# A four-image scan network on one core: a deeper head, spaced background loads and a staggered end

## The chip, the cores and the metric

The kernel runs on one core of a Trainium2 chip. The core has five engines that run side by side: TensorE (PE in the profile, with PEld for its weight loads), VectorE (DVE), ScalarE (ACT), GpSimd (POOL) and SyncE (SP), which here only starts transfers. Each engine works through its own list of instructions in order. On-chip data lies in SBUF, results of matmuls in PSUM, inputs and scratch tensors in DRAM; transfers between them are asynchronous.

The metric is the device time of one execution in microseconds (us). The kernel before takes 5479.21 us, the median of three runs from 5474.62 to 5479.99.

## The reference

The input is 4 images of 64 x 64 positions with 96 channels. Per image there is a convolution branch with a state-space scan, then a linear attention and a feed-forward layer with rounding. Cut to what matters here:

```python
xp, z = split(bilinear(group_norm(x), W_in, s_in, b_in))     # signs of x times signs of W
t = conv3x3(sign(xp + move), s * sign(conv_W)) + biases      # 192 -> 192 channels
t = where(t >= 0, t, prelu * t) + rp_b1 + xp
xconv = silu(t)                                              # "u" in the kernel
x_hwwh = stack([xconv by rows, xconv by columns])            # and both reversed: 4 directions
xs = concat([x_hwwh, flip(x_hwwh)])
dts, Bs, Cs = split(bilinear(xs as rows of 192, Wl, sl, bl)) # per direction
h = exp(dt * A) * h + (dt * u) * B                           # along 4096 positions, 192 x 16 states
y = sum_n(h * C) + D * u
y = y_0 + flip(y_2) + (y_1 + flip(y_3)) by columns turned back to rows
y = layernorm(y) * silu-like gate of z;  x = x + bilinear(y, W_out, ...)
t = x + attention(layernorm(x))      # linear: q (k^T v), summed over the whole image
t = t + ffn(layernorm(t))            # 96 -> 384 -> 96, rounded to small float formats
```

Two things shape the kernel. The attention sums k^T v over the whole image, so the end of an image has a first pass (sums), a small middle product and a last pass. And the scan of a direction needs, for each position, the rows B, C and dt that are made from the whole convolution.

## The kernel before

The main loop, `Scans.run`, goes through 1536 pieces (4 images, 4 directions in the order 1, 3, 0, 2, 4 stretches of 1024 positions, 6 groups of 32 channels, 4 groups of states). Each piece is a decay on ScalarE, an input product on GpSimd, a scan on VectorE, a product with C on VectorE or GpSimd, and a reduction on TensorE. All other work, the head of the next images and the end of the finished ones, is written as Python generators; after each piece one step of them is emitted, so that it fills the engines' gaps:

```python
for i in range(n):
    self.loads(i)
    ...
    if i % NQ == 1:
        while KORD[self.pieces[i][1]] == 2 and self.pieces[i][0] not in c.turned:
            next(back)                       # forced: the turned sums are needed now
        self.load_sums(i)
    self.carry(i - 1); self.decay(i + 1)     # ScalarE
    self.reduce(i - 4)                       # TensorE
    self.inject(i + AHEAD); self.late_product()   # GpSimd
    self.scan(i)                             # VectorE
    c.later.tick()                           # stores that were put off
    ...
    interleave(lanes)                        # one step of the next deltas (dps)
    next(back, None)                         # one step of the background work
```

The background, in `run`: for each image b in turn, wait until its second direction is scanned, turn that direction's result from columns to rows (`turn`), make the head of image b + 2 (`prologue`), then sums, middle and last of image b.

```python
scans = Scans(c)
...
    for b in range(NB):
        while not scans.done(b, 2): yield
        yield from turn(c, b)
        if b + 2 < NB: yield from prologue(c, b + 2)
        e = ends[b]; e.open()
        yield from e.sums(e.lane)
        if b + 1 < NB:
            yield from e.middle(); yield from e.last(e.lane); e.close()
...
drain([e.middle()])                                       # image 3, after the scans
drain([e.last(ln) for ln in [e.lane] + more])             # four lanes, one step each in turn
```

Image 0's head has no scan beside it (`alone`). It runs in turn with `weights()`, which prepares all weights: `interleave([made, first])`. Its convolution works on 16 parts of 512 columns (two halves h of the channels, eight q). Each part, in four steps and an ending:

```python
for n, part in enumerate(parts + [None]):
    for s in range(4):
        if part: ...                               # 15 matmuls "cv", four to a step
        if ahead and s == 0: next(ahead[0])        # projection of a later part: matmuls ix, iz
        if ahead and s == 2: next(ahead.pop(0), None)   # its signs tp, sz on ScalarE
        if prev and s == 0: pz = pz * S_X + v; pz = r * oma + pz     # VectorE, two products
        if prev and s == 1: sign(ph, pq, pz); e = exp(-pz)           # ScalarE
        if prev and s == 2: e = ln(1 + e); e = exp(-e)               # ScalarE
        if prev and s == 3: u = pz * e                               # VectorE
                            c.later.store(ud, u); by_columns(ph, pq, u)   # GpSimd copy into ut
        yield
    if part:
        v = cv * acs + acb                         # VectorE
        r = relu(cv * csc + cbias)                 # ScalarE
        pz = winT.T @ xsT                          # TensorE, "cz"
        prev = (h, q, pz, v, r, nm)
```

`sign` stores its 32-row pieces with `c.later.store(xgw[...], sg[m::3, :])`, a transfer started by SyncE two steps later. The tile ut for u by columns comes from a pool that closes at the end of the convolution.

Then the rows stage turns xg into xr (13 copies, banks used in turn of two), makes B, C and dt (acc, eight row products), and writes bcd and the signs sgd. `Scans.start` begins with loads of u and of the B rows (bc), makes the first deltas and sends them on as dl.

The parts of the background with a load ahead of a use:

```python
load_x(c, b, xts); yield; yield                    # prologue: then the column sums (csum)
...
c.later.flush()                                    # end of the convolution: last signs to xg
with tc.tile_pool(name=f"rw_{b}", bufs=1) as rw:   # rows: xg read, xr written at once
...
ts = [load(*part) for part in parts[:3]]           # turn: three loads ahead of the copies (yh)
...
if (ci, part) == (NCH - 1, 0) and k != KORD[-1]:   # deltas: signs of the next direction,
    self.load_signs(b, KORD[KORD.index(k) + 1])    #   but not of the next image
...
tt = ln.tts[n % 2]; nc.sync.dma_start(tt[0:96, :], c.td[b][...])   # last: then the product "at"
```

In the last pass each chunk of 512 columns goes through: at, x2, fc, square, fv, rstd, t8, three hidden products hp, fy, fo, ft, out. A step is about one of these.

Of the kernel before, what the change touches and what calls it, by code (L numbers as in the profile page):

```python
# [53 lines left out]
def hybrid_kernel(ctx: ExitStack, tc: tile.TileContext, a: dict, out: bass.AP):  # L54
# [108 lines left out]
    def weights():  # L163
# [110 lines left out]
        part = temp("part", [96, 2, 2])  # L274
        for i, cut in enumerate(cuts):
            nc.scalar.activation(cwA.rearrange("p t d -> p (t d)")[:, cut], cfa[i], AF.Sign, saturate=False)
            nc.scalar.activation(cwB[:, lines[i]], cfb[i], AF.Sign, saturate=False)
            for h in range(2):
                nc.vector.tensor_reduce(part[:, h, i : i + 1], cwn[h][i], AX.X, ALU.add, apply_absolute_value=True)
        nc.vector.tensor_tensor(csc, part[:, :, 0], part[:, :, 1], ALU.add)  # L280
        nc.vector.tensor_scalar(csc, csc, 1.0 / (9 * DN), None, ALU.mult)
        yield

        nc.vector.tensor_tensor(cbias, pv[:, :, CONV_B], pv[:, :, RP0], ALU.add)
        nc.vector.tensor_tensor(acs, pv[:, :, PRELU], csc, ALU.mult)
        nc.vector.tensor_tensor(acb, pv[:, :, PRELU], cbias, ALU.mult)
        nc.vector.tensor_tensor(acb, acb, pv[:, :, B_X], ALU.add)
        nc.vector.tensor_tensor(acb, acb, pv[:, :, RP1], ALU.add)
        nc.vector.tensor_scalar(oma, pv[:, :, PRELU], -1.0, 1.0, ALU.mult, ALU.add)
        for h in range(2):  # L290
            nc.gpsimd.tensor_scalar(omad[:, h], i96, oma[:, h : h + 1], None, ALU.mult)
        yield
# [5 lines left out]
        for o in range(2):  # L298
# [18 lines left out]
            yield  # L317

# [87 lines left out]

def load_x(c, b, xts):
    src = c.a["x"][b].rearrange("(i p) e -> p i e", p=128)
    for q, t in enumerate(xts):
        c.nc.sync.dma_start(t, src[:, 8 * q : 8 * q + 8, :])  # L410
# [41 lines left out]
def run(c):  # L452

    made, first = c.weights(), prologue(c, 0, c.xts)
    lanes = [made, first]
    next(made)
    for _ in range(6):
        next(first)
    while (0, 1) not in c.ready:
        interleave(lanes)  # L460
        c.later.tick()
    assert made not in lanes
    scans = Scans(c)
    ends = [Epilogue(c, b, scans) for b in range(NB)]

    def back():
# [3 lines left out]
        for b in range(NB):  # L470
            while not scans.done(b, 2):
                yield
            yield from turn(c, b)
# [5 lines left out]
            if b + 1 < NB:  # L479
                yield from e.middle()  # L480
                yield from e.last(e.lane)
                e.close()
# [15 lines left out]
    more.append(e.fourth_lane())  # L498
    drain([e.middle()])
    drain([e.last(ln) for ln in [e.lane] + more])  # L500
# [3 lines left out]
def prologue(c, b, xts=None):  # L504
# [11 lines left out]
    with tc.tile_pool(name=f"xg_{b}", bufs=1) as xgp:  # L516
# [3 lines left out]
        with tc.tile_pool(name=f"cv_{b}", bufs=1) as cvp:  # L520
# [7 lines left out]
            if xts is None:  # L528
# [5 lines left out]
                yield  # L534
                yield

            csum = bank("csum", 0)[0:1, 0 : 4 * DM]
            for i in range(0, NT, 4):
# [4 lines left out]
                if i % 8 == 4:  # L543
                    yield
            row = f32("csr")[0:1, 0 : 4 * DM]
# [98 lines left out]
            utp = sub.enter_context(tc.tile_pool(name=f"ut_{b}", bufs=1))  # L644
            uts = {}

            def by_columns(h, q, u):


                per = 2 if alone and h else 4  # L650
                if q % per == 0:
                    uts[h] = utp.tile([96, IW, 8 * per], F32, name=f"ut{h}{q}_{b}", tag=f"ut{h if alone else 0}")
# [3 lines left out]
                if q % per == per - 1:  # L656
                    rows = slice(8 * (q + 1 - per), 8 * q + 8)
                    c.later.store(c.utd[b][h].rearrange("p (w h) -> p w h", h=IH)[:, :, rows], ut, after=1)

            def sign(h, q, pz):  # L660
# [5 lines left out]
                for m in range(3):  # L666
                    g0 = 64 * (m // 2) + 32 * h
                    c.later.store(xgw[g0 : g0 + 32, m % 2, 128 * q : 128 * q + 128], sg[m::3, :])

            for n, part in enumerate(parts + [None]):  # L670
                if part:
                    h, q = part
                    nm = f"{h}{q}"
                    if alone:
                        ps = c.p.dA.tile([128, CH], F32, name=f"cv{nm}_{b}", tag="dA")[0:96, 0:512]
                    else:
                        ps = bank("cv" + nm, 0)[0:96]
                for s in range(4 if alone else 5):
                    if part:
                        per = 4 if alone else 3  # L680
                        for tp, w, dy, dx in taps[per * s : per * s + per]:
# [4 lines left out]
                    if alone and ahead:  # L686
                        if s == 0:
                            next(ahead[0])
                        elif s == 2:
                            next(ahead.pop(0), None)  # L690
# [3 lines left out]
                    if prev:  # L694
                        ph, pq, pz, v, r, pn = prev
                        if s == 0:
                            if alone:
                                c.vec.scalar_tensor_tensor(pz, pz, pv[:, ph, S_X : S_X + 1], v, ALU.mult, ALU.add)
                                c.vec.scalar_tensor_tensor(pz, r, c.oma[:, one(ph)], pz, ALU.mult, ALU.add)
                            else:  # L700
                                nc.scalar.mul(pz, pz, pv[:, ph, S_X : S_X + 1])
                        elif s == 1 and not alone:
# [3 lines left out]
                        elif s == (1 if alone else 2):  # L706
# [4 lines left out]
                        elif s == (2 if alone else 3):  # L711
                            nc.scalar.activation(e, e, AF.Ln, bias=1.0)
                            nc.scalar.activation(e, e, AF.Exp, scale=-1.0)
                        elif s == (3 if alone else 4):
# [4 lines left out]
                            if alone:  # L719
                                by_columns(*turned)  # L720
                                turned = None
                    yield
                if part:
                    v, r = f32("v" + nm)[0:96], f32("r" + nm)[0:96]
                    if alone:
                        nc.vector.tensor_scalar(v, ps, c.acs[:, one(h)], c.acb[:, one(h)], ALU.mult, ALU.add)
                    else:
                        nc.scalar.activation(v, ps, AF.Identity, scale=c.acs[:, one(h)], bias=c.acb[:, one(h)])
                    nc.scalar.activation(r, ps, AF.Relu, scale=c.csc[:, one(h)], bias=c.cbias[:, one(h)])  # L729
                    pz = bank("cz" + nm, n % 2 if alone else 1)[0:96]  # L730
# [11 lines left out]

        with tc.tile_pool(name=f"rw_{b}", bufs=1) as rw:
# [7 lines left out]
            gw = g2.bitcast(F32)  # L751
            for o in (1, 0):
# [10 lines left out]
                for n in range(13):  # L763
# [3 lines left out]
                    if n < 8:  # L767
                        ps = bank(f"xa{o}{n}", n % 2)
# [3 lines left out]
                    elif n < 12:  # L772
                        ps = bank(f"xb{o}{n}", n % 2)
# [9 lines left out]
                for gh in range(2):  # L783
                    groups = slice(32 * gh, 32 * gh + 32)
                    prev = None
                    for n in range(5):
# [9 lines left out]
                        if n < 4:  # L796
                            acc = prev = bank(f"acc{o}{gh}{n}", n % 2)
# [36 lines left out]
                for x, k in enumerate((o, o + 2)):  # L834
                    nc.sync.dma_start(gw[:, x, 16:64], c.sgd[b][k].rearrange("(p f) -> p f", p=128))
                    yield
# [25 lines left out]
def turn(c, b):  # L862
# [9 lines left out]
    with tc.tile_pool(name=f"tn_{b}", bufs=1) as tn:  # L872
        ts = [load(*part) for part in parts[:3]]
        for n, (h, q) in enumerate(parts):
            if q == 0:
                yh = tn.tile([96, L], F32, name=f"yh{h}_{b}", tag=f"yh{h}")
# [5 lines left out]
            if n + 3 < len(parts):  # L882
                ts.append(load(*parts[n + 3]))
# [5 lines left out]
class Epilogue:  # L889


    def __init__(self, c, b, scans):
        self.c, self.b, self.scans = c, b, scans

        self.todo, self.rest = list(range(NQ8))[::-1], list(range(NQ8))
# [83 lines left out]
    def loads(self, ln, q, names):  # L979
        c, b = self.c, self.b  # L980
        cols = slice(512 * q, 512 * q + 512)
        for nm in names:
# [6 lines left out]
            c.nc.sync.dma_start(t[0:96], src[..., cols])  # L989
# [162 lines left out]
    def last(self, ln):  # L1152
# [21 lines left out]
        x1 = residual(nxt[0]) if nxt else None  # L1174
        while nxt:
# [73 lines left out]
class Scans:  # L1249
# [20 lines left out]
    def done(self, b, n):  # L1270

        return self.at > (b * NK + n) * NPC + SETTLE
# [14 lines left out]
    def prepare(self, spare=None):  # L1287
# [11 lines left out]
        if (ci, part) == (NCH - 1, 0) and k != KORD[-1]:  # L1299
            self.load_signs(b, KORD[KORD.index(k) + 1])  # L1300
# [168 lines left out]
    def evacuate(self, i):  # L1469
# [6 lines left out]
        c.nc.scalar.copy(t, y[:, :, ::-1] if k >= 2 else y)  # L1476
        at = CH * (NCH - 1 - ci if k >= 2 else ci)
# [4 lines left out]

    def start(self):
# [3 lines left out]
        w = [p.w.tile([128, CH], F32, name=f"w_s{x}", tag="w") for x in range(8)]  # L1487
        t, d2, us = w[4:6], w[6], w[2:4]
# [177 lines left out]
```

## Time and profile before

The page says of the whole span of 5482.3 us:

| engine | busy us | share |
|---|---|---|
| VectorE | 5016.3 | 91% |
| GpSimd | 4938.7 | 90% |
| ScalarE | 3615.3 | 66% |
| TensorE, matmuls | 3415.9 | 62% |

By time the span falls into three: a head until about 257 us, in which image 0 is prepared; the scans until about 5352 us; and the end of image 3, about 130 us. In the page's 40 slices of 137 us GpSimd shows 2, 3, then 9 throughout, and 0 in the last.

An average over these three says little about any of them, so the reading is by stretches: the busy time of each engine in a window, and in the timeline the idle time ahead of an instruction with what ended it. A line such as "A L1 <- B x L2: total, times, longest" in the view of waits says that instructions A at line 1 were released by B writing x at line 2, for so many us in total. Line L423 is the helper through which the scans and products of VectorE and GpSimd are issued, L442 the helper of put-off stores, L994 that of the end's matmuls.

### The profile page before, as it was taken

The page shows a single profiled execution, that of the slowest core. Times are in us where ns is not written, and L with a number is a line of the kernel's source. Part 1 is how long each engine was busy: PE and PEld are TensorE (multiplying, and loading weights), DVE is VectorE, ACT ScalarE, POOL GpSimd, SP SyncE. Part 2 cuts the span into 40 slices and gives each one's busy share as a digit, 9 for nine tenths or more (in the row PEclk, how much of TensorE's full clock was granted, in tenths as well). Part 3 has the DMA queues.
Part 4 walks back from the last instruction along what each step waited for, and adds up shares of the span by engine and source line. Part 5 has one row for each costly group of instructions (what it writes and reads, how often), then busy time and mean ns, then how long its engine had stood idle before and what let it go on. Part 6 is the DMA issues. An engine that isn't in the chain of part 4 may idle for free. (4 is left out here: it accounts for less than half of the span.)

```text
span 5482.3 us, 62080 instructions
## 1 busy us (share of the span) xinstructions
PE 3415.9 (62%) x20083; PEld 1355.4 (25%) x20083; DVE 5016.3 (91%) x3171; ACT 3615.3 (66%) x5648; POOL 4938.7 (90%) x2245
## 2 busy tenths in 40 slices
PE   6456665467656776657764676664676664444577
PEld 3222222122222222222222222221232221111233
DVE  4499999899999999999999999999999999999994
ACT  4467777687766667778777666776666775555554
POOL 2399999899999999999999999999999999999990
PEclk7666776678766777767886787766787666666777
DMA  4565666767666666576665665667666565665652
GB/s 82 128 211 171 207 207 199 228 213 213 195 200 201 189 208 204 196 244 213 217 199 181 216 198 186 216 192 225 217 218 187 189 204 194 195 211 194 212 175 62
DMA packets 624219, 1069.06 MB, mean 195 GB/s; under 512 B 237307, under 2 KB 355092, under 8 KB 622100
## 3 DMA queue, kind: packets, MB, share of 16 engines
q1 hardware_dynamic: 623236, 1065.07, 62.2%
q8 instruction: 157, 2.57, 0.2%
q14 instruction: 170, 1.39, 0.1%
q10 hardware_dynamic: 656, 0.02, 0.0%
HBM read 830.01 MB, written 228.56 MB: 193 GB/s over the span
## 5 line engine op out<-in xcount | busy, mean ns | idle before, releaser
L423 POOL TENSOR_TENSOR w<-dl,bc 128x1024 f32<-128x1024 f32 x1524 | 3550.0, 2355 | 88.0 <-PE yp L1462 52.8
L1389 ACT ACTIVATE dA<-dl,anm 128x1024 f32<-128x1024 f32 x1524 | 1701.1, 1116 | 486.0 <-DVE w L423 284.5
L423 DVE TENSOR_TENSOR_SCAN dA<-dA,cy,w 128x1024 f32<-128x1024 f32 x725 | 1698.6, 2343 | 107.8 <-ACT dA L1389 94.2
L423 POOL TENSOR_TENSOR w<-h,bc 128x1024 f32<-128x1024 f32 x570 | 1341.4, 2353 | 127.8 <-DVE h L423 113.6
L1462 PE MATMUL yp<-w,sum 128*32 128x256 f32 x12288 | 1254.7, 505 | 323.8 <-ACT pd L1343 235.0
L423 DVE TENSOR_TENSOR w<-dA,bc 128x1024 f32<-128x1024 f32 x966 | 1183.1, 1225 | 65.4 <-DMA bc<-bcd 4.0
L423 DVE TENSOR_TENSOR_SCAN h<-dA,cy,w 128x1024 f32<-128x1024 f32 x427 | 999.2, 2340 | 17.4 <-ACT dA L1389 16.7
L1462 PEld LDWEIGHTS yp<-w,sum 128*32 128x32 f32 x12288 | 316.9, 127 | 1401.0 <-issue 731.4
L1431 ACT COPY cy<-dA 128x1 f32<-128x1 f32 x725 | 114.0, 157 | 753.2 <-DVE w L423 751.3
L423 DVE TENSOR_TENSOR_SCAN dA<-dA,w 128x1024 f32<-128x1024 f32 x241 | 550.2, 2283 | 34.7 <-ACT dA L1389 28.0
L1324 PE MATMUL dps<-gT,wdz 128*128 128x64 fp8e5 x1008 | 116.6, 316 | 399.9 <-ACT ys L1476 373.9
L423 DVE TENSOR_TENSOR_SCAN h<-dA,w 128x1024 f32<-128x1024 f32 x143 | 325.9, 2279 | 18.8 <-POOL w L423 16.1
L1337 PE MATMUL dps<-sp,ident 128*128 128x512 f32 x378 | 268.5, 799 | 96.2 <-ACT dps L1333 96.1
L1467 PE MATMUL yp<-ya,back 128*128 128x256 f32 x576 | 226.3, 511 | 0.0
L682 PE MATMUL cv<-tp,cwA 128*96 128x512 fp8e5 x576 | 197.9, 467 | 33.3 <-ACT r L729 30.9
L1324 PEld LDWEIGHTS <-wdz 128*128 128x128 fp8e5 x1008 | 95.6, 153 | 479.2 <-issue 451.7
L1324 PE MATMUL dps<-gT,wdy 128*128 128x64 fp8e5 x504 | 58.7, 318 | 221.0 <-ACT ys L1476 220.8
L1431 ACT COPY cy<-h 128x1 f32<-128x1 f32 x427 | 79.3, 186 | 133.5 <-DVE h L423 132.8
L994 PE MATMUL yc<-eys,mean 96*96 96x512 f32 x240 | 141.4, 744 | 29.5 <-DVE vks L423 14.4
L1329 ACT ACTIVATE pd<-dps,dbias,pvd 128x512 f32<-128x512 f32 x189 | 143.9, 761 | 20.8 <-PE dps L1324 20.5
L1467 PEld LDWEIGHTS yp<-ya,back 128*128 128x128 f32 x576 | 117.6, 236 | 119.9 <-issue 88.2
L1330 ACT ACTIVATE sp<-dps,dbias,pvd 128x512 f32<-128x512 f32 x189 | 144.8, 766 | 0.0
(363 smaller groups left out, 4457.2 us busy)
## 6 DMA issues: line engine op xcount, KB each, us to landing
dl<-dld SPq DMA_DIRECT2D x762, 512.0 KB
bc<-bcd SPq DMA_DIRECT2D x512, 512.0 KB
dld<-pd SPq DMA_DIRECT2D x126, 512.0 KB
yd<-ys SPq DMA_DIRECT2D x768, 64.0 KB
dld<-pd SPq DMA_DIRECT2D x126, 256.0 KB
ya<-yd SPq DMA_DIRECT2D x192, 128.0 KB
pu<-ud SPq DMA_DIRECT2D x32, 512.0 KB
pu<-utd SPq DMA_DIRECT2D x31, 512.0 KB
```

The lines of the kernel that those rows point to most:

```text
L423: return getattr(self.eng, name)(out, *args, **kw)
L682: nc.tensor.matmul(ps, w[:, 96 * h : 96 * h + 96], tp[:, 8 * q + dy : 8 * q + dy + 8, dx : dx + IW], start=(w is taps[0][1]), stop=(w is t ...
L994: self.c.nc.tensor.matmul(ps, w, x, start=(i == 0), stop=(i == len(pairs) - 1))
L1324: nc.tensor.matmul(pv[:, s], wd[:, k, s], gT[:, :, c0 : c0 + 16], start=(s == 0), stop=(s == 7))
L1329: nc.scalar.activation(d[:, 0], ps, AF.Abs, scale=sc, bias=bi)
L1330: nc.scalar.activation(t, ps, AF.Relu, scale=sc, bias=bi)
L1337: nc.tensor.matmul(ps, c.ident, t, start=False, stop=True, skip_group_check=True)
L1389: c.nc.scalar.activation(t, self.dlt[i // NQ][0], AF.Exp, scale=c.anm[:, g, NQ * KORD[e] + q : NQ * KORD[e] + q + 1])
L1431: self.c.nc.scalar.copy(self.carries[g, q], h[:, CH - 1 : CH])
L1462: c.nc.tensor.matmul(y[32 * x : 32 * x + 32, g % 2, :], c.sum4, prod[:, 256 * x : 256 * x + 256], start=(q == 0), stop=(q == NQ - 1 and no ...
L1467: c.nc.tensor.matmul(y[:, g % 2, :], w, src, start=False, stop=(n == len(more) - 1))
```

## The change

It has six parts, named in the order of the program.

1. **Head.** The first image's head gets two steps for each step of the weights, and the sums of the convolution weights (`scales`) come after the row weights. The convolution becomes three parts deep: while part n is in the matmuls, part n-1 is in the products, sign and exp, and part n-2 in ln, exp and u. The signs are sent to xg by GpSimd's own transfers, ut lies in the pool w, and the rows stage of image 0 uses four banks. The loads of B and u for the first scan are asked for before the signs are worked on (`loads_ahead`).
2. **Column sums, rows, turning, last pass.** Further steps lie between a load and its first use. `turn` loads five parts ahead and keeps one yh tile instead of two.
3. **Order of turning.** If the next image's second direction is nearly scanned, it is turned before this image's middle and last.
4. **Signs of the next image** are loaded ahead, as those of the next direction were.
5. **Sums of the last image.** The last two groups' result goes from the SBUF tile to the lanes directly, not through yd.
6. **End.** The four lanes fetch their first chunk before the middle product, start two steps apart, and take the chunks in the other order.

The core of the diff:

```diff
-    while (0, 1) not in c.ready:
-        interleave(lanes)
+    next(made)
+    while (0, 1) not in c.ready:
+        interleave([first])
         c.later.tick()
+        if (0, 1) not in c.ready:
+            interleave(lanes)
+            c.later.tick()
 ...
-            yield from turn(c, b)
+            if b not in c.turned:
+                yield from turn(c, b)
 ...
+                if scans.done(b + 1, 2, 20):
+                    while not scans.done(b + 1, 2):
+                        yield
+                    yield from turn(c, b + 1)
                 yield from e.middle()
 ...
+    c.later.flush()
+    last = [e.last(ln) for ln in [e.lane] + more]
+    for g in last:
+        next(g)
     drain([e.middle()])
-    drain([e.last(ln) for ln in [e.lane] + more])
+    drain([apart(2 * x, g) for x, g in enumerate(last)])
 ...                                             # prologue, column sums
-                yield
-                yield
+                for _ in range(4):
+                    yield
 ...
+            if not alone:
+                yield
             row = f32("csr")[0:1, 0 : 4 * DM]
 ...                                             # sign()
-                    c.later.store(xgw[g0 : g0 + 32, m % 2, 128 * q : 128 * q + 128], sg[m::3, :])
+                    if alone:
+                        nc.gpsimd.dma_start(dst, sg[m::3, :])
+                    else:
+                        c.later.store(dst, sg[m::3, :])
 ...                                             # new: alone_parts()
+                        if s == 0:
+                            if ahead: next(ahead[0])
+                            if mid: ...           # both products of part n-1
+                        elif s == 1 and end: ...  # ln, exp of part n-2
+                        elif s == 2:
+                            if ahead: next(ahead.pop(0), None)
+                            if mid: ...           # sign, exp of part n-1
+                        elif s == 3 and end: ...  # u, its store, by_columns of part n-2
 ...                                             # rows
+        if not alone:
+            for _ in range(3):
+                yield
         with tc.tile_pool(name=f"rw_{b}", bufs=1) as rw:
+                if fast and j % 4 > 1:            # row_bank: two more banks
+                    return c.p.ps.tile([128, 512], F32, name=f"{nm}_{b}", tag=f"y{j % 2}")
 ...
+                    if fast and x:
+                        c.loads_ahead()
 ...                                             # turn
-        ts = [load(*part) for part in parts[:3]]
+        ts = [load(*part) for part in parts[:5]]
+        yield
+        yield
 ...
+                for _ in range(4 * h):
+                    yield
 ...                                             # last
+        if not self.alone:
+            yield
+            yield
         while nxt:
 ...                                             # signs
-        if (ci, part) == (NCH - 1, 0) and k != KORD[-1]:
-            self.load_signs(b, KORD[KORD.index(k) + 1])
+        if (ci, part) == (NCH - 1, 0):
+            then = (b, KORD[KORD.index(k) + 1]) if k != KORD[-1] else (b + 1, KORD[0])
+            if (then[0], then[1] % 2) in self.c.ready:
+                self.load_signs(*then)
```

## The prediction

> **What bounds the kernel now.** I read first the page's busy table and slices, then the busy time by stretches, then the waits of VectorE, ScalarE and TensorE inside the scan, and last the timelines of the head and of the end. The stretches give the frame. Columns after the stretch: length, then PE, PEld, DVE, ACT and POOL busy with their counts, granted clock, DMA share, GB/s.
>
> ```profile
> 63.00:177.00 114.00, 76.06 (x288) 37.19 (x288) 51.12 (x92) 68.77 (x109) 16.08 (x16) 0.83 0.41 67
> ...
> 270.00:5340.00 5070.00, 3164.16 (x18948) 1228.35 (x18948) 4833.37 (x2885) 3419.86 (x5326) 4852.69 (x2115) 0.73 0.64 203
> ...
> 5405.00:5483.00 78.00, 58.79 (x195) 24.97 (x194) 37.97 (x73) 38.69 (x65) 0.00 (x0) 0.74 0.22 61
> ```
>
> From 270 to 5340 us VectorE is busy 95% and GpSimd 96%: they share the scans and products, and the change leaves the count of every compute instruction on both as it was. There only their idle time, 5070 - 4833 = 237 us, can be won. In the head (0 to 257 us) and the end (5352 to 5482) no engine is full; chains of dependent steps set the time.
>
> Inside the scan these waits are not the normal hand-over between the engines (total us, times, longest):
>
> ```profile
> DVE dA L423 <- ACT dA L1389: 122.3, 94, 9.4
> ...
> ACT yh L878 <- DMA yt<-yd: 32.0, 12, 6.2
> ...
> ACT xr L765 <- DMA utd<-ut: 21.8, 3, 8.1
> ...
> PE dps L1324 <- DMA gT<-gTd: 23.9, 3, 12.2
> ...
> PE csum L539 <- DMA xt<-in_x: 18.2, 2, 10.7
> ...
> PE at L994 <- DMA tt<-td: 15.7, 3, 10.8
> ```
>
> ScalarE and TensorE are in order. A background instruction that waits for a DMA holds the decay (dA) or the reduction behind it, and the scan then waits for that. The VectorE timeline, its last number the idle time before the instruction, gives each a size:
>
> ```profile
> 810.72 2.35 DVE L423 TENSOR_TENSOR_SCAN h<-dA,cy,w 128x1024 f32<-128x1024 f32 x1 [5.98 <-ACT dA L1389]
> ...
> 1454.65 2.36 DVE L423 TENSOR_TENSOR_SCAN dA<-dA,cy,w 128x1024 f32<-128x1024 f32 x1 [9.39 <-ACT dA L1389]
> ```
>
> At 811 us ScalarE had stood for the first row copy; at 1455 us TensorE had stood 12.2 us for signs of the next image.
>
> **What the Trainium skill says.** "Perfetto Trace Analysis", Optimization Strategy: find the gaps of the engine that should be full and what would release them earlier. The list above is that, and the trace agrees that such gaps exist, but they are 52 us of 237. "TensorE: Matmul & The Clock Gate", Part 1: matmuls run at half rate until TensorE has been busy for some microseconds. The trace agrees: six convolution matmuls take 2.62 us at 104 us and 1.46 us at 111 us. "DMA: Bandwidth & Descriptors", Anatomy of one DMA: a transfer issued by GpSimd costs about 2 us fixed; no transfer of this kernel is issued there yet, so the trace can't say. The same page, Issuing engines are not separate DMA queues: a second issuing engine saves only issue time. Here issue time is not small, the SyncE queue spends 6 us on one store:
>
> ```profile
> 172.84 6.02 SPq L442 DMA_DIRECT2D ud<-u  x1
> 178.95 1.77 SPq L442 DMA_DIRECT2D xg<-sg  x3
> ```
>
> **Part 1, the head.** In the convolution of image 0 each part of 512 columns is one chain: v and r, two products, sign and exp, ln and exp, u, and only then the next v. ScalarE shows the empty places:
>
> ```profile
> 119.72 0.77 ACT L729 ACTIVATE r<-cv,cbias,csc 96x512 f32<-96x512 f32 x1 [1.53 <-DVE v L726]
> 121.48 0.59 ACT L662 ACTIVATE sg<-cz 96x512 fp8e5<-96x512 f32 x1 [0.99 <-DVE cz L423]
> ```
>
> The value v starts at 111.14, 118.88 and 125.76 us: 7.3 us a part on average, and 5.7 us for the last five, which have no projection beside them. After, ln/exp/u belong to the part before the previous. By distance of starts, ScalarE needs r 0.70, sign 0.50, exp 0.47, ln 0.65, exp 0.66, sz 0.68 and tp 0.78 or 1.58, on average 4.8 us; TensorE needs 15 x 0.215 + 3 x 0.21 = 3.9 us if warm, VectorE 3.0. So 5 us with projection and 3.8 without.
>
> The first parts now share their time with the weights: the image's steps run twice for each step of the weights, so some ten VectorE casts of weights (1.2 us each) and GpSimd's 4.1 us spreads fall between parts 0 and 5. I give these six 7.5 us each. The first v waits for the row-weight signs and for GpSimd's clearing of tp, both as before until about 41 us, then five projections of some 2 us with transposes between: v of part 0 at about 58 us, 5 us earlier than its 63.2. Then 6 x 7.5 + 6 x 5 + 3 x 3.8 = 86, so the last v at 144 in place of 170.9: 27 us won.
>
> Then the rows. Before, the last sign ends at 174.1 us, the signs' transfer waits behind two stores, and the first row copy also waits until the store of ut has landed (same memory): 188.25 us, 14 us after the sign. After, GpSimd issues the three transfers and ut lies in another pool; 3 issues of an estimated 1 us and 2 us to land, worked out from that page, and 1 us of TensorE make some 6 us: 8 won. Four accumulators in place of two let the eight row products go at 1.0 rather than 1.4 us each: 3 won. The B rows (4 x 512 KB) are asked for before the signs rather than after, so the 512 KB tiles of delta, which landed 7 us after issue, share the bandwidth with less: 5 won. Head: 27 + 8 + 3 + 5 = 43 us.
>
> **Part 2, inside the scan.** VectorE's gaps, from its timeline: rows 5.98, 3.73, 5.02; turning 5.13, 1.71, 4.25; column sums 2.50, 3.78; signs 9.39, 2.03, 2.97; the last stage's read of td 5.80. Sum 52.3 us. The added steps (one step is one piece, 5070/1530 = 3.3 us) put 7 to 16 us between load and use, about the longest wait. GpSimd was idle in the same places, so most counts fully; I take 70%, 37 us, since two-step moves leave remainders and a forced burst of background work might appear. In the order of instructions no piece carries more than five background ScalarE instructions, before and after, so I expect none. The small gaps of 1.3 us (some seventy) stay.
>
> **Part 3, the end.** From 5405 us eight chunks go through four lanes in lockstep, two rounds, the second 35 us. Per chunk TensorE needs at, fc, fv 3 x 0.86, hp 1.1, fy 1.4, ft 1.25: 6.3 us, so 8 x 6.3 = 50 us, plus 5 to fill and 9 for the last lane to drain: 64 in place of 77. The loads asked for before the middle matrix save the 1.7 us wait of the first product within that. The last chunk's sums go from SBUF to SBUF, not through DRAM; the load behind "DMA ln1b<-yd" took 6.08 us on the chain, I take 2 off. End: 15, less 2 for lanes that collide: 13 us.
>
> Sum: 43 + 37 + 13 = 93; 5479 - 93 = 5386.
>
> **Rivals.** (a) GpSimd becomes the head's bound: three issues and a 1.05 us copy per part; were an issue 1.5 us, 5.6 us a part in place of 5 and 3.8, the head's gain falls by 15 us, and the time is 5401. For it: its transfers stand in line with weight spreads. Against: it was busy 16 of 114 us. (b) The DVE gaps close but turn up elsewhere, because GpSimd (96%) is then the bound or the later background work piles up before a deadline: the turning of image 1 now ends one piece before its sums are loaded. Then part 2 gives 10 us and the time is 5413. Against: both engines idled together in most gaps. (c) The weights leave the head's path altogether: parts 0 to 5 at 5 us too, 15 us more, and all of part 2: 5479 - 58 - 52 - 15 = 5354.
>
> **Range and chances.** Part errors of some 15, 15 and 6 us make about 22 together, more with an unseen wait: 5350 to 5425. Faster by over 2% needs under 5369.6, 16 us more than I sum, a 0.27 chance. Slower by over 2% would need a wholly new stall: 0.02.
>
> **What would show it.** Right: the last v near 144 us, the scan steady near 215 us, the six waits above gone or under 2 us each, VectorE busy over 95.8% between, some 118 us from the last scan to the end. Wrong: v still 7 us apart or GpSimd idle nowhere in the head; a new wait on transfers from GpSimd; VectorE gaps over 3 us at other lines; VectorE busy time itself changed.

## The result

| | before | after |
|---|---|---|
| time, us (median; lowest to highest) | 5478.45 (5474.62 to 5479.99) | 5408.55 (5406.08 to 5412.43) |
| ratio to before, 95% interval | | 0.987 (0.986 to 0.989) |
| last v of the convolution of image 0 | 170.9 | 159.3 |
| first scan | 237.7 | 214.7 |
| first to last scan | 5115.4 | 5068.6 |
| last scan to the end | 129.2 | 122.2 |

The lower four rows are start times in the two profiled executions. The kernel became 70 us faster, 1.3%; 93 us were predicted. Of the 77 us between the two profiles (5482.3 and 5405.6 us), 23 come from the head, 47 from the scan and 7 from the end, where 43, 37 and 13 were expected.

**The profile after.** Busy time by stretches: length, then PE, PEld, DVE, ACT and POOL with counts, granted clock, DMA share, GB/s. They are the convolution, the steady scan and the last pass.

```profile
59.00:160.00 101.00, 72.88 (x337) 38.66 (x336) 55.99 (x96) 62.77 (x102) 43.33 (x91) 0.86 0.49 68
247.00:5270.00 5023.00, 3166.26 (x18948) 1229.61 (x18948) 4831.42 (x2885) 3423.61 (x5326) 4851.59 (x2114) 0.73 0.65 205
5335.00:5406.00 71.00, 55.28 (x194) 24.36 (x194) 37.20 (x73) 39.10 (x64) 0.00 (x0) 0.81 0.20 55
```

In the scan VectorE does the same 2885 instructions in the same 4831 us; its idle time fell from 237 to 5023 - 4831 = 192 us. The gain in the scan is those 45 us. VectorE's gaps of 1.9 us or more in these stretches were 14 with 59.0 us in sum; 7 with 21.1 us are left. In the convolution no engine is full: ScalarE is busy 63 of 101 us.

VectorE's waits in the scan (total us, times, longest):

```profile
DVE dA L435 <- ACT dA L1505: 86.1, 75, 2.8
...
DVE w L435 <- DMA bc<-bcd: 8.1, 5, 5.8
```

The wait for the decay fell from 122.3 to 86.1 us and its longest from 9.4 to 2.8. That for B rows (bc) grew from 4.0 to 8.1 us. Of the five waits of ScalarE and TensorE named in the prediction, those before yh, xr and dps are gone; two remain, without a long wait for a decay behind them:

```profile
PE csum L566 <- DMA xt<-in_x: 20.3, 3, 8.4
PE at L1105 <- DMA tt<-td: 7.5, 1, 7.5
```

**The head.** VectorE's timeline, at the place where the convolution stops (the last number is the idle time before the instruction and what ended it):

```profile
119.09 0.81 DVE L757 TENSOR_SCALAR v<-cv,acs,acb 96x512 f32<-96x512 f32 x1
122.84 0.69 DVE L435 TENSOR_TENSOR u<-cz,e 96x512 f32<-96x512 f32 x1 [0.43 <-ACT e L737]
133.50 0.81 DVE L757 TENSOR_SCALAR v<-cv,acs,acb 96x512 f32<-96x512 f32 x1 [9.98 <-DMA ud<-u]
140.43 0.69 DVE L435 TENSOR_TENSOR u<-cz,e 96x512 f32<-96x512 f32 x1 [4.41 <-DMA ud<-u]
```

An arithmetic instruction waits for a store: v, r, sg, e and u share the eight buffers of one pool, and a new v needs a buffer whose u has been written out. What kept the store back is on the SyncE queue at the same time (start, us that the queue was held, count):

```profile
103.49 5.30 SPq L391 DMA_DIRECT2D sbR<-in_sl_bc  x1
...
113.23 17.02 SPq L397 DMA_DIRECT2D anm<-in_al  x24
130.35 1.52 SPq L454 DMA_DIRECT2D ud<-u  x3
```

The last step of the weights asks for 12 small pieces of row scales (sbR) and 24 of decay rates (anm). From 103 to 130 us the queue issues nothing else, the first of them held for 5.3 us behind a store of ut (102.85 us); the stores of u go out after it. The theory for the missing 15 us of the convolution (T1) is this queue; the rival (T2) is the weights' casts and GpSimd's spreads, which the prediction had put into the first six parts.

### The profile page after: what moved, and what is told of

Read it like the earlier page. It is cut to its first block, busy times and chain, and to the rows that moved or that the text cites. A ratio compares the mean times of both kernels' runs of the same rounds, so it can differ in the third digit from the quotient of the medians.

```text
span 5405.6 us, 62146 instructions
## 1 busy us (share of the span) xinstructions
PE 3405.6 (63%) x20083; PEld 1351.6 (25%) x20083; DVE 5013.4 (93%) x3171; ACT 3617.6 (67%) x5648; POOL 4962.1 (92%) x2293
## 3 DMA queue, kind: packets, MB, share of 16 engines
q1 hardware_dynamic: 633028, 1063.89, 63.7%
## 5 line engine op out<-in xcount | busy, mean ns | idle before, releaser
L435 DVE TENSOR_TENSOR w<-dA,bc 128x1024 f32<-128x1024 f32 x966 | 1183.2, 1225 | 69.9 <-DMA bc<-bcd 8.1
L780 PE MATMUL cv<-tp,cwA 128*96 128x512 fp8e5 x432 | 155.2, 478 | 39.1 <-ACT r L812 38.3
L1105 PE MATMUL yc<-eys,mean 96*96 96x512 f32 x240 | 140.1, 738 | 45.6 <-DVE vks L435 23.9
L1583 PEld LDWEIGHTS yp<-ya,back 128*128 128x128 f32 x576 | 116.8, 234 | 119.0 <-issue 90.4
```

Source lines behind the costliest of these rows:

```text
L435: return getattr(self.eng, name)(out, *args, **kw)
L780: nc.tensor.matmul(ps, w[:, 96 * h : 96 * h + 96], tp[:, 8 * q + dy : 8 * q + dy + 8, dx : dx + IW], start=(w is taps[0][1]), stop=(w is t ...
L1105: self.c.nc.tensor.matmul(ps, w, x, start=(i == 0), stop=(i == len(pairs) - 1))
L1583: c.nc.tensor.matmul(y[:, g % 2, :], w, src, start=False, stop=(n == len(more) - 1))
```

## The experiments

Each is the changed kernel with one edit, or, where the text says so, with several. The rows show the start of the last v, of the first and of the last scan, the stretch between them, and last scan to end, all in the profiled execution; the time is the median, the ratio is to the kernel before.

| kernel | time | ratio (95%) | last v | first scan | last scan | between | end |
|---|---|---|---|---|---|---|---|
| after | 5408.6 | 0.987 (0.986 to 0.989) | 159.3 | 214.7 | 5283.4 | 5068.6 | 122.2 |
| e1 | 5398.9 | 0.986 (0.984 to 0.987) | 146.9 | 203.2 | 5280.6 | 5077.5 | 122.2 |
| e2 | 5427.9 | 0.991 (0.990 to 0.992) | 176.0 | 230.7 | 5309.6 | 5079.0 | 122.2 |
| e3 | 5447.5 | 0.994 (0.993 to 0.996) | 157.5 | 213.1 | 5323.4 | 5110.2 | 122.0 |
| e4 | 5412.4 | 0.988 (0.987 to 0.989) | 159.5 | 215.2 | 5286.9 | 5071.7 | 123.4 |
| e5 | 5420.2 | 0.989 (0.988 to 0.991) | 154.8 | 211.1 | 5293.2 | 5082.1 | 122.2 |
| e6 | 5413.5 | 0.988 (0.987 to 0.990) | 156.0 | 216.5 | 5282.6 | 5066.1 | 120.7 |
| e7 | 5396.7 | 0.986 (0.984 to 0.987) | 155.5 | 212.0 | 5281.1 | 5069.2 | 115.7 |
| e8 | 5396.0 | 0.985 (0.983 to 0.986) | 143.4 | 199.6 | 5272.5 | 5073.0 | 122.4 |
| e9 | 5388.0 | 0.984 (0.982 to 0.985) | 143.7 | 196.1 | 5273.9 | 5077.9 | 112.1 |
| e10 | 5395.2 | 0.985 (0.984 to 0.986) | 143.8 | 196.5 | 5257.5 | 5061.0 | 130.8 |
| e11 | 5420.6 | 0.990 (0.988 to 0.991) | 165.2 | 224.2 | 5294.5 | 5070.3 | 119.0 |
| e12 | 5373.9 | 0.981 (0.980 to 0.983) | 142.5 | 195.2 | 5259.0 | 5063.8 | 112.2 |

The scan of after, e1, e2, e4, e6, e7, e8, e9 and e11 is the same code, and its length runs from 5066 to 5079 us. So a difference of up to 13 us between the scans of two profiles can be chance; VectorE's waits for B rows alone run from 8.1 us (after) to 17.1 us (e9) in these nine. In the same way the last v runs from 154.8 to 159.5 us in the six profiles with the convolution of after (after, e3 to e7). The kernel before had medians of 5477.5 to 5480.2 us beside these runs, so a difference of some 3 us between two times says nothing. Effects in the head and at the end are therefore read from their own stages, effects in the scan from medians and from the waits themselves.

**e1: the small loads earlier.**

```diff
+    def small_loads(): ...   # the 12 loads of sbR and 24 of anm
-        ...                  # the same loads, at the end of weights()
                 del ahead[:4]
+                c.small_loads()
```

> The changed kernel, with only the 12 loads of sbR and the 24 loads of anm put on the SyncE queue right after the eight xb stores (where that queue is idle from 47 to 70 us) instead of after the last step of the weights (103 to 130 us). T1, the SyncE queue held by these loads keeps u, v and r tiles from coming free: the 10 us stall of v at 123.5 us goes, the last v starts near 147 rather than 159.3 us, the first scan near 203 rather than 214.7, and the time falls by 8 to 12 us, to some 5398. T2, the weights' casts and GpSimd's spreads bind and the stall only shows what they left: the last v and the time stay within 3 us of the changed kernel.

The last v came at 146.9 us and the first scan at 203.2, as T1 had it; the time fell by 9.6 us. VectorE's timeline shows the 10 us stop gone, but shorter ones of the same kind left:

```profile
123.69 0.69 DVE L437 TENSOR_TENSOR u<-cz,e 96x512 f32<-96x512 f32 x1 [2.11 <-DMA ud<-u]
...
130.75 0.81 DVE L760 TENSOR_SCALAR v<-cv,acs,acb 96x512 f32<-96x512 f32 x1 [2.94 <-DMA ud<-u]
```

**e8: and u of image 0 stored by GpSimd.**

```diff
-                            c.later.store(c.ud[b][eh][:, 512 * eq : 512 * eq + 512], u)
+                            nc.gpsimd.dma_start(c.ud[b][eh][:, 512 * eq : 512 * eq + 512], u)
```

> The kernel with the small loads early (5399 us, last v at 146.9 us), and besides the 16 stores of u of image 0 issued by GpSimd rather than SyncE, so that they do not stand behind the stores of ut (6144 runs of 64 bytes, 5 to 6 us of queue each). T1, these stores are what keeps tiles of the f pool from coming free in the second half of the convolution: v every 4 to 5 us there, the last v near 140, the time 5 to 8 us less than 5399. T2, GpSimd's issues (0.5 us each) and the tiles' other users bind: within 2 us. T3, GpSimd falls behind with its spreads and copies: 3 us or more longer.

From the sixth step on v is 3.8 to 5.0 us apart. The six parts in the middle of the convolution (from the seventh v to the thirteenth) took 27.0 us, in e1 32.8, in the six profiles with the convolution of after 40.9 to 42.8; e9, e10 and e12, which keep both edits, have 27.0 too. So in that stage T1 came, 5.8 us. The last v came only 3.4 us before e1's (143.4 us), because the first six parts took 46.6 us here and 43.9 there, and the time fell by 3.0 us, which is not clear of chance. GpSimd had the room: in the changed kernel its 48 transfers of signs cost 0.50 us of issue each (busy us, mean ns, then idle time before):

```profile
L708 POOL DMA_DIRECT2D xg<-sg x48 | 23.8, 501 | 63.8 <-ACT sg L700 63.8
```

**e2: the convolution two parts deep again.** The loop of the kernel before stands in place of alone_parts.

> The changed kernel, with only the convolution of image 0 back to the loop of the kernel before (two parts deep); the order of the weights, signs by GpSimd, the tiles of ut and everything behind stay changed. T1, the third part of depth pays where nothing is stalled (5 of 16 parts), 2 us each, and is eaten where the queue holds the tiles: the last v comes 5 to 12 us later, the time is 5 to 12 us longer. T2, depth is what the head's gain of 12 us at the last v consists of, or more: 20 us longer. T3, the head is bound by the weights and the queue alone: no difference.

The last v came 16.7 us later, the time was 19.3 us longer: T2. The third part of depth is worth more than the head's whole gain at the last v (11.7 us): with it undone the last v came 5 us later than in the kernel before. The first v came 5.0 us earlier than there and the way from it to the last took 10.0 us more; which of the other changes cost that was not taken apart. By thirds: the first six, middle six and last three parts took 58.1, 42.8 and 16.9 us in e2, 45.6, 42.7 and 11.8 in after, 48.0, 42.6 and 17.2 in before. Depth pays in the first and last third; in the middle one, where the queue is held, it gave nothing, as T1 had it. And in e2 the same loads of anm held the queue for 16.3 us from 110 us on, but v stayed 6.8 to 7.7 us apart and VectorE waited for no store. The stop belongs to both together, the held queue and the deeper loop.

**e11: signs of image 0 sent by SyncE again.**

```diff
-                        nc.gpsimd.dma_start(dst, sg[m::3, :])
+                        c.later.store(dst, sg[m::3, :])
```

> The changed kernel with only the signs of image 0 sent by SyncE again (behind the stores of u and ut) rather than by GpSimd. T1, the 8 us between last sign and first row copy are worth having GpSimd send them: the row copies start some 10 us later after the last v (8.7 us with GpSimd), the sg tiles come free later besides, the time is 8 to 15 us longer. T2, the place of ut in another pool was what freed the rows, and GpSimd gives nothing: within 3 us.

The time was 12.0 us longer: T1 by size. But only 3.2 us of it lie between last v and first row copy (177.10 - 165.21 = 11.9 us, in after 167.96 - 159.28 = 8.7). The last v itself came 5.9 us later, because now the sg tiles stood behind the anm loads too and v stopped for 23 us at 104 us.

**e6: B rows and u asked for after the signs.** The call of first_loads goes back into start. The edit kept the new order inside it, so u stays behind the four B rows; the text below says otherwise, and on that it is wrong.

> The changed kernel with only the early B rows and u of the first pieces undone: they are asked for again after the signs, with u of the first part ahead of the four B rows. T1, u behind 2 MB of B rows is what made the stretch from the sign columns to the first scan 2 us longer: that stretch falls from 24.5 to 22 to 23 us, the time is 0 to 3 us shorter. T2, the early B rows did win landing time for delta as predicted and something else cost 7 us: the stretch grows to 28 to 30 us.

From the sign columns (first write of gT, 187.46 us) to the first scan it took 29.1 us, in after 24.5 (from 190.20), in before 22.3 (from 215.40). T2's number came: in this order the early asking wins 4.6 us. What costs more than that, 6.8 us against before, is u behind 2 MB of B rows. So the early asking mostly makes good what the order costs: with u first it is 22.3 us late (before) and 21.8 early (e9 below), a gain of 0.5. The time was 4.9 us longer. VectorE's wait for u, here and in after:

```profile
203.33 0.69 DVE L435 TENSOR_TENSOR w_s<-w_s,w_u 128x512 f32<-128x512 f32 x1 [6.88 <-DMA w_u<-utd]
```
```profile
201.45 0.69 DVE L435 TENSOR_TENSOR w_s<-w_s,w_u 128x512 f32<-128x512 f32 x1 [2.25 <-DMA w_u<-utd]
```

**e3: all changes inside the scan undone.**

> The changed kernel with all of its changes inside the scan undone: steps before column sums, rows and the last stage's loop, the depth, steps and place of the turning, signs of the next image loaded ahead. Head and end stay changed. T1, the 12 gaps are what the 46.8 us between first and last scan start consist of: the stretch grows from 5068.6 to some 5115 us and the time by 42 to 52 us. T2, part of it comes from elsewhere (the order of the head's loads, the last chunk's sums): under 35 us.

The time was 38.9 us longer and the stretch between the scans 5110.2 us, 41.6 more than in after. 39 us lies between T1's 42 and T2's 35, nearer to T1. After's scan is the second shortest of the nine equal ones, so of the two numbers the median's is the better. VectorE's gaps of 1.9 us or more are back at 53.6 us (12), from 21.1.

**e5: only the signs of the next image late again.** The condition on load_signs is that of before.

> The changed kernel with only the loading ahead of the next image's signs undone. T1, the gaps that this load made (9.39, 2.03, 2.97 us: 14.4 in sum) come back nearly whole: VectorE waits of 2 to 9 us at each start of an image, the time 10 to 14 us longer. T2, they come back in the trace but GpSimd or the next burst of background work takes up the slack: 5 us or less.

11.6 us longer: T1. The gap at the second image's start is back, and the one at the third's; at the fourth's it is 4.0 us, where after has 2.0:

```profile
1402.74 2.35 DVE L435 TENSOR_TENSOR_SCAN h<-dA,cy,w 128x1024 f32<-128x1024 f32 x1 [5.81 <-ACT dA L1504]
...
2685.46 2.36 DVE L435 TENSOR_TENSOR_SCAN dA<-dA,cy,w 128x1024 f32<-128x1024 f32 x1 [5.56 <-ACT dA L1504]
```

**e4: the four last lanes in lockstep.** apart(2 * x, g) became g.

> The changed kernel with its four last lanes in lockstep again (no steps between their starts); the loads ahead, the order of the chunks and the ys tiles sent within SBUF stay. T1, the stagger is the end's 6 us: the stretch from the middle product to the end grows from 70 to 76 us, the time by 5 to 7. T2, the loads ahead of the middle product are what gives the 6 us and the stagger nothing, since TensorE runs cold while one lane is alone: the time within 2 us.

Last pass from its first product at: 71.2 us, in after 69.9, in before 76.5 with its wait for td. The stagger gives 1.3 us of 6.6. The rest lies with what e4 keeps, the loads before the middle product above all; no run undoes these alone. By size that is T2. Its reason holds only in part. Ten us of the pass in after, then two such stretches of e4 (clock third from the end):

```profile
5345.00:5355.00 10.00, 9.39 (x13) 2.36 (x12) 3.68 (x7) 4.81 (x9) 0.00 (x0) 0.50 0.14 39
```
```profile
5349.00:5359.00 10.00, 7.30 (x19) 2.41 (x18) 3.55 (x6) 8.87 (x15) 0.00 (x0) 0.98 0.00 1
5359.00:5369.00 10.00, 7.19 (x16) 1.96 (x14) 9.54 (x21) 7.25 (x13) 0.00 (x0) 0.51 0.00 0
```

Staggered, TensorE is busy 9.4 of 10 us and gets through 13 instructions at half the clock. But the lockstep falls to half the clock too, only later. Over the whole pass the mean granted clock is 0.81 in after, 0.83 in e4 and 0.73 in before, so the stagger is not what brings half the clock about.

**e7: four products computed again, to fill TensorE's holes.** The results are overwritten by the same values or by later ones.

```diff
                 mm(ps, [(self.ms[2], tt)])
+                if warm:                       # first lane, first chunk
+                    mm(bank("wa", 1)[0:96], [(self.ms[2], tt)])
 ...
+                mm(bank("wb", 0)[0:96], [(c.mean96, x2)])     # after fc, if warm
 ...
+                mm(ps, [(c.on96, t)])          # twice before fv, if warm
```

> The changed kernel with four products of the first lane's first chunk computed again (one after at, one after fc, two before fv, into banks that are overwritten afterwards), so that TensorE has no hole between 5335 and 5343 us. T1, the end won only 5 of 11 us in its last pass because the granted clock falls to 0.50 while one lane is alone: the f32 products of 5345 to 5360 us take 1.02 rather than 2.02 us and the last pass falls from 70 to some 65 us, the time by 3 to 6. T2, the lanes' chains bound it and not TensorE's clock: the pass stays at 69 to 72 us.

The last pass took 63.4 us, 6.5 less, and the granted clock was 1.00 from 5325 to 5390 us. The same pair of products in after and here:

```profile
5351.45 2.02 PE L1105 MATMUL ln1ps<-ln1w,mean 96*96 96x512 f32 x2 [0.35 <-DVE ln1w L435]
```
```profile
5346.54 1.10 PE L1105 MATMUL ln1ps<-ln1w,mean 96*96 96x512 f32 x2 [0.56 <-DVE ln1w L435]
```

T1 is shown, by the trace; the two medians are 12 us apart, more than the pass explains, with overlapping intervals of their ratios.

**e9: what helped, joined.** e8 and e7, and in first_loads the two loads of u moved ahead of the loop of B rows.

> What helped, joined: small loads early, stores of u of image 0 by GpSimd, the four products computed again in the last pass, and u of the first pieces asked for ahead of the early B rows (the order, not the place, is new). T1, the parts add up: last v near 143.5, the stretch from the sign columns to the first scan 22 rather than 24.5 to 25 us since u no longer waits behind the B rows, last pass 63 to 64 us, the time 5386 to 5390. T2, B rows that land later make the first products wait instead: the stretch stays at 24 to 25 us, the time 5389 to 5392.

5388.0 us; sign columns to first scan 196.06 - 174.22 = 21.8 us, last pass 63.7 us: T1. The gains of head and end stand next to each other. Of the end's 10.1 us, 3.9 lie ahead of the last pass and are no part's gain: that stretch is 52.3 us in after and 48.3 in e11 too, with the same code.

**e10: two spreads inside the scan.** Two steps after each of the four loads of x, and one step between the two products of yc.

> The same, and two steps in the scan besides: the four loads of x of a later image two steps apart rather than together (they hold the SyncE queue for 10 us near 2435 us, with B rows behind them), and one step between the two halves of the 7 us of products for yc in the sums (ScalarE waits for them twice 2.7 us, with the decay behind it). T1, these waits stand on the path of the scan: the VectorE waits for bc near pieces 676 to 772 and the four near pieces 1133 to 1181 fall from some 22 us to under 8, the time 8 to 14 us below that of the run beside it. T2, the slack is taken elsewhere or the later background meets a deadline: within 3 us, or longer.

T2. The stretch between the scans did fall, to 5061.0 us, but the background had four more steps in each later prologue and one per chunk of the sums, and the turning of image 1, which in after ends one piece before piece 672, no longer did. ScalarE and then VectorE there:

```profile
2429.63 7.71 ACT L982 COPY yh<-yt 96x512 f32<-96x512 f32 x8 [12.03 <-DMA y<-yh]
```
```profile
2438.65 2.29 DVE L438 TENSOR_TENSOR_SCAN h<-dA,w 128x1024 f32<-128x1024 f32 x1 [17.58 <-ACT cy L1562]
```

Eight copies run in one piece, VectorE stands for 17.6 us, and the end is 18.7 us longer (130.8 against 112.1) because sums of the last image are left over for it.

**e12: x one load a step, no step added.**

```diff
-                load_x(c, b, xts)
-                for _ in range(4):
+                for q in range(4):
+                    load_x(c, b, xts, q)
                     yield
```

> The joined kernel (small loads early, u of image 0 by GpSimd, u ahead of the early B rows, products repeated in the last pass), and the four loads of x of each later image one a step in place of four together and four steps after: no step is added, so the turning of image 1 still ends before its deadline at piece 672, and the step between the products of yc is left out. T1, the waits for B rows near pieces 676, 748, 772 and 1108 (6.9, 1.7, 2.5, 2.4 us in the joined kernel's trace) come from the queue that the four loads hold: they fall to under 4 us in all, and the time is 5 to 10 us below 5388. T2, these waits are a matter of the DMA engines' load (0.92 to 0.94 busy there) and not of the queue: the time stays within 3 us of 5388.

14.2 us below e9, or 11.5 when each is taken from the kernel before that ran beside it, more than T1 asked for; 5373.9 us is the fastest kernel here. The SyncE queue in e9, then in e12:

```profile
2419.32 9.49 SPq L424 DMA_DIRECT2D xt<-in_x  x4
2430.99 0.55 SPq L1482 DMA_DIRECT2D bc<-bcd  x1
```
```profile
2416.24 0.42 SPq L425 DMA_DIRECT2D xt<-in_x  x1
2422.87 0.64 SPq L1483 DMA_DIRECT2D bc<-bcd  x1
2423.56 3.46 SPq L425 DMA_DIRECT2D xt<-in_x  x2
```

In e9 a B row waits behind four loads that hold the queue for 9.5 us, and VectorE then waits 6.85 us for B at 2439 us. In e12 a B row goes between them, and no wait of VectorE for B is longer than 1.6 us (3.4 us in all, after 17.1). That is T1, and 3.4 lies below all nine profiles with the scan of after. But 17.1 is the highest of the nine (8.1 to 17.1), so that the 13.7 us between the two sums nearly equal the gain in time is partly chance.

## Why the prediction was right, and where its parts were not

The range held, but the middle was 23 us low, and two of the three parts missed by 20 and 6 us. That the time still lay inside owes something to a range 75 us wide. Of the signs that would show it right, these did not come: the last v (159.3 for 144), the six waits gone or under 2 us (three are still up to 2.8, 7.5 and 8.4 us long), and the steady scan near 215 us (from 257 in before less the head's 23, some 234; that the first scan starts at 214.7 us is another mark).

**Convolution, 27 us: 11.7 measured.** The starting point was right (v of part 0 at 58; 59.2 measured), so were the six parts beside the weights (6 x 7.5 = 45; 45.6) and the last three (3 x 3.8 = 11.4; 11.8). The failed term is the middle six: 6 x 5 = 30 was a count of engine time, and it measured 42.7, as long as in the kernel before (42.6). Missing in it was the SyncE queue as a thing that can be full, though the prediction itself had quoted a store that held it for 6 us. e1 and e8 show it: with the queue freed step by step the six take 32.8 and 27.0 us, and the last v comes at 143.4, where 144 was predicted. In the kernel before, the same loads of anm held the queue for 16 us from 76 us on, and v kept its 6.8 to 7.7 us beside them, as it did in e2. The deeper loop holds the tiles of one more part; that more than eight buffers would help was not tried.

**Last sign to first row copy, 8 us:** from last v to first row copy 17.3 became 8.7, so 8.6 won; right in size. e11 puts 3.2 of it on GpSimd's sending. The rest goes with a wait for the store of ut that is gone (no run puts ut back alone); in before:

```profile
188.25 0.58 ACT L765 CAST xr<-xa 128x512 bf16<-128x512 f32 x1 [12.32 <-DMA utd<-ut]
```

**Row banks, 3 us:** first copy to sign columns 27.2 became 22.2, 4.9 won, but mostly in another step than the one named. From the first copy to the first row product 7.8 became 4.7 us, which the prediction left out; from there to the last sign, the step it named, 15.1 became 13.2.

**B rows early, 5 us: -2.2 measured.** The claimed mechanism, delta landing sooner beside less traffic, is worth at most 1.0 us (issue to first use 8.15, then 7.2), and e6 has 7.3 with B rows asked for late. The step that failed is the order: the change also puts u behind the B rows (e6, e9). In the sum: 11.7 + 8.6 + 4.9 - 2.2 = 23.0, against 43.

**Scan, 37 us: 39 by e3.** Signs, 70% of 14.4 = 10, measured 11.6 (e5). The mechanism was right: waits put apart from their loads. The 70% was a guess that came out well, and the list of gaps was not whole: it left out three of 3.0, 2.9 and 2.5 us (at 1853, 3263 and 3341 us in before), where ScalarE waits for the products of yc. The change does nothing for these; after has four of the kind, 11.0 us in all, at 3964, 4047, 4092 and 4133 us. All such waits of ScalarE, before and after (total us, times, longest):

```profile
ACT sq L1054 <- PE yc L994: 63.4, 49, 2.7
```
```profile
ACT sq L1165 <- PE yc L1105: 69.0, 48, 2.9
```

Rival (b) is there in small: these waits grew by some 3 to 6 us, and the gap at the loads of x from 3.8 to 5.8 us (e12 removes it). e10 is rival (b) in full, when steps are added past what the deadline allows. Right "over 95.8%": 4831/5023 = 96.2%.

**End, 13 us: 7 measured.** The pass was put at 50 + 5 + 9 = 64 us. The term that failed is the 50, a count at full clock: the pass ran at a mean granted clock of 0.81 and took 69.9. The Trainium skill, "TensorE: Matmul & The Clock Gate", Part 1, which the prediction had cited for the head, says that a TensorE not kept busy falls to half rate. The traces agree (2.02 against 1.10 us for the same pair of products), and e7 with its holes filled took 63.4. The lanes' stagger is not the cause by itself, since the lockstep of e4 has 0.83. The 2 us for the sums of the last chunk weren't there: last scan to the moment when at could start is 52.7 us before and 52.3 after.

**Rival (a)**, GpSimd bound by its issues, fell: 0.50 us each, not 1.5 (and not the 1 us estimated; landing, put at 2 us, took 2.3 us by the median). Its 15 us were wrong besides: its own terms, 5.6 in place of 5 and 3.8 us, give 6 x 0.6 + 3 x 1.8 = 9. **Rival (c)** fell too: the first six parts stayed at 7.6 us each.

## What to carry to other kernels

When a chain is made deeper it holds more buffers, and each is free only when its store has been issued: count the issuing queue's time in that stretch like an engine's, with every small load that merely happens to stand there. Move such loads to where the queue is idle, and let urgent small ones go between large ones. Steps that spread background work are paid from a budget that ends at its next deadline, and a short pass of small dependent products can run at half the granted clock for long stretches (20 of 70 us here): read the clock of the stage before counting its products at full speed. A saving inside a long stretch needs several runs: nine profiles of the same scan differed by 13 us here.

## What the runs showed of the hardware

Here a DMA of many short runs held the queue for the next issue. Each store of ut is 6144 runs of 64 bytes; its own issue took 0.6 us, and the one after it was held:

```profile
131.96 0.61 SPq L454 DMA_DIRECT2D utd<-ut  x1
132.66 5.33 SPq L454 DMA_DIRECT2D ud<-u  x1
```

The 24 loads of anm, single values at a time, took 0.71 us each (17.02 / 24), and four loads of x 2.4 us each (9.49 / 4), where one that found the queue free took 0.42 us (e12). The Trainium skill, "DMA: Bandwidth & Descriptors", Issuing engines are not separate DMA queues, calls the issue time, which is all that a second issuing engine saves, usually small beside the transfer itself. Here it stood in a chain that set the time: with u on GpSimd's queue rather than behind the ut stores, the middle six parts of the convolution took 5.8 us less (e8), and with the signs there the kernel was 12 us faster (e11). GpSimd's own issue, 0.50 us for 32 runs of 512 bytes, was no dearer than SyncE's for the same pieces in before (1.77 / 3 = 0.59 us).

Being busy did not by itself bring TensorE's clock back: from 5340 to 5360 us of after it was busy 18.2 of 20 us, with gaps of 0.3 to 0.8 us between its groups, at a granted clock of 0.50.
